# Forty of the experts' batch slots as seven-product items instead of group steps, in a kernel of shared and selected experts on one Trainium2 core

## The chip, the core and the metric

The kernel runs on one core of a Trainium2 chip. The metric is the device time of one execution in microseconds, as a median of several runs. The engines work side by side, each through its own list of instructions: PE (TensorE, matmuls), DVE (VectorE), ACT (ScalarE), POOL (GpSimd) and SP (SyncE, which here issues nearly all DMAs).

## What is computed

For 128 batches of 64 tokens with 256 features, two shared experts and one of five selected experts (hidden width 1024) are applied, mixed by a gate, added to the input, and then one diffusion step is made along both axes.

```python
def _dense(x, wi_, wo_):
    return jax.nn.relu(x @ wi_) @ wo_
...
s0 = _dense(x, swi[0], swo[0])
s1 = _dense(x, swi[1], swo[1])
wi_sel = wi[type_label]
wo_sel = wo[type_label]
h = jax.nn.relu(jnp.einsum('bsd,bdf->bsf', x, wi_sel))
eo = jnp.einsum('bsf,bfd->bsd', h, wo_sel)
gate_in = jnp.concatenate([eo[:, 0], s0[:, 0], s1[:, 0]], axis=-1)
w = jax.nn.softmax(jax.nn.relu(gate_in @ g1) @ g2, axis=-1)
...
return eo * w[:, 0] + s0 * w[:, 1] + s1 * w[:, 2]
```

Then `x = x + that`, and `x = x + zX*lap_x + zY*lap_y + zR*x*(1-x)`. The input has x in (128, 64, 256); `type_label` is one number per batch, known only at run time.

## The kernel before

**Precision.** Each fp32 operand is split into a high part (ACT copies it to a rounded type) and a low part (source minus high, on DVE or POOL; `split`, line 110). A product is three matmuls: high by high, high by low, low by high. In the second layer the high hidden part meets high and low weights in one matmul 512 wide, and the low hidden part meets the high weights in one 256 wide.

**Shared experts: items.** Tokens are taken as eight pairs of tiles; a tile is four steps of all 128 batches, 512 tokens, so a pair has 1024. An item n is one pair with one of the two shared experts (n = 2p + e, 16 items). An item has four units q, each for two of the eight hidden blocks of 128. A unit (`unit`, line 555) makes its 2 x 2 block product in seven block products in place of eight (Strassen-Winograd): the weight blocks A11, A12, A22 and sums S1 to S4, the token blocks B11, B21, B22 and sums T1 to T4, each times 3 matmuls, 21 matmuls of 512 columns per unit. The products go to PSUM tiles pa, pb and pd. pb takes several products one on top of the other, and between them ACT copies it out: to seed it from pa, then to u2, then to u3 (group `u` in the profile). TensorE's next product into pb waits for that copy.

Between the products of unit q stand "gaps": the second layer's matmuls of the preceding unit (`tile_a`) or, in unit 0, of the last rows 2 and 3 of the preceding item (`tile_b`, whose rows 0 and 1 stand at the item's end). `evacuate` (line 673) takes a finished row of 128 tokens out of PSUM: for items 0 and 1, ACT copies and DVE adds into the tiles `sh`, which stay in SBUF until the gate's weights exist; later items add onto yb.

Besides, a unit has four places for other work, its hooks. `at(k, ...)` (line 907) puts work at hook k, which is unit k // 4, place k % 4; 16 and 17 are after the last unit. Hook 0 of a unit stands behind its first gap, hook 1 behind the second gap, hook 2 behind the third. In order of the program a unit is: pa product, seed copy, gap, hook 0, S2 and A12 products, u2 copy and one hidden block, gap, hook 1, S3 and S1 products, u3 copy, gap, hook 2, A22 and S4 products, three more hidden blocks, hook 3.

ACT, DVE, POOL and PE keep the order of the program in this part (`in_order`, `keep_in_program_order`), and SP always does. A hook thus fixes where an instruction stands in the list of its engine. An engine may run ahead of the others as far as its own inputs allow, and if one instruction waits, all behind it on that engine wait too.

**Weights of items 0 and 1** come raw (`load_ws`) and are prepared on the fly: `prepare(u, k)` has POOL make S1 to S4 (`sum_wi`, four small sums) at k, splits the A blocks at k + 2 and the S blocks at k + 3 (`split_wi`), saves them to DRAM (`keep_wi`), and splits W-out at k + 4 (`split_wo`). The split W-out of all eight units stays in SBUF for the whole run (`wpool`). `again(0)` and `again(1)`, at hook 17 of items 0 and 1, prepare the first two units' S blocks, which item 0 did without. From item 2 on the split weights come back from DRAM (`load_wi`).

**Order of the batches.** `order_batches` (line 232), run in four steps at hooks of items 0 and 1, sorts the batches by expert into slots in units of four and writes a table `tab`: the batch of every slot and the expert of every unit of four. There are two classes: expert runs in eights come first, fours after. SP reads addresses from the table.

**Selected experts: groups.** After item 1, `stream` runs 19 groups that always exist: 14 of eight batches (512 tokens) and 5 of four. Two more run only if the table says so. A group uses plain products: 48 matmuls of 512 columns (`up`), then 32 of 512 and 32 of 256 (`down`); its results go to DRAM (`eo_d`). `load_group_x` (line 338) issues one DMA of 64 KB per batch. Group 0 is loaded at hook 12 of item 1 (`load_first_group`) and split at hook 16.

**Items 2 to 15** follow, with the gate in item 2, the results of the experts gathered from `eo_d`, and the diffusion in the hooks.

Of the kernel before, what the change touches and what calls it, by code (L numbers as in the profile page):

```python
# [8 lines left out]
F32 = mybir.dt.float32  # L9
# [7 lines left out]
P = 128  # L17
# [7 lines left out]
NBIG = (B // NB - NE + 2) // 2  # L25
NSURE = B // NB + 1 - 2 * NBIG
GROUPS = [(2 * NB * g, 2 * NB) for g in range(NBIG)] + [(u * NB, NB) for u in range(2 * NBIG, NU)]
# [6 lines left out]
LAG = 2  # L34
NWARM = 8
# [7 lines left out]
def cond_resid_kernel(ctx: ExitStack, tc: tile.TileContext, xg, xs, xn, itok, z, we, ws, g1, g2, out):  # L43
# [8 lines left out]

    nc = tc.nc
    const = ctx.enter_context(tc.tile_pool(name="const", bufs=1))
    wpool = ctx.enter_context(tc.tile_pool(name="wpool", bufs=1))
# [8 lines left out]
    eo_d = dram.tile([NSLOT * NT, ST * D], F32, name="eo_d")  # L64
    wi_d = [dram.tile([P, 2, 7, P], F32, name=f"wi_d{i}") for i in range(2 * NQ)]
# [56 lines left out]

    def split_wo(u):
        wop[u] = wpool.tile([P, 2, 2, D], F32R, name=f"wo{u}")
        split(wop[u][:, :, 0, :], wop[u][:, :, 1, :], wsr[u][:, :, 256:512], vec)

# [40 lines left out]

    def sum_x(p, i, eng):

        b11, b12, b21, b22 = (xraw[p, k, l] for k in range(2) for l in range(2))  # L170
        if i == T1:
            xsum[p, T1] = slot2(f"xt{p}_1")
            eng.tensor_tensor(xsum[p, T1], b12, b11, ALU.subtract)
        elif i == T2:
            xsum[p, T2] = slot2(f"xt{p}_2")
            eng.tensor_tensor(xsum[p, T2], b22, xsum[p, T1], ALU.subtract)
        elif i == T3:
            xsum[p, T3] = slot2(f"xt{p}_3")
            eng.tensor_tensor(xsum[p, T3], b22, b12, ALU.subtract)
        else:  # L180
            xsum[p, T4] = slot2(f"xt{p}_4")
            eng.tensor_tensor(xsum[p, T4], b21, xsum[p, T2], ALU.subtract)

    def split_x(p, i, eng):
        src = {B11: (0, 0), B21: (1, 0), B22: (1, 1)}
        src = xraw[(p,) + src[i]] if i in src else xsum[p, i]
        x = xop[p, i] = slot4(f"x{p}_{i}")
        split(x[:, 0, :], x[:, 1, :], src, eng)
# [43 lines left out]
    def order_batches():  # L232
# [7 lines left out]
        gps.memset(ones, 1.0)  # L240
        io_i = const.tile([P, NSLOT], I32, name="io_i")
# [22 lines left out]
        pad = const.tile([P, NE], F32, name="pad")  # L264
        vec.tensor_copy(pad, cntb)
        vec.tensor_scalar(cntb, cntb, -2 * NB, None, ALU.bitwise_and)

        big = const.tile([P, NE], F32, name="big")
        vec.tensor_copy(big, cntb)
        vec.tensor_sub(pad, pad, big)  # L270

        base = const.tile([P, 2 * NE + 1], F32, name="base")
        vec.memset(base, 0.0)
        for e in range(2 * NE):
            size = (big if e < NE else pad)[:, e % NE : e % NE + 1]
            vec.tensor_add(base[:, e + 1 : e + 2], base[:, e : e + 1], size)
        inbig = const.tile([P, NE], F32, name="inbig")
        vec.tensor_tensor(inbig, rank, big, ALU.is_lt)
        shift = const.tile([P, NE], F32, name="shift")
        vec.tensor_sub(shift, base[:, NE : 2 * NE], big)  # L280
        vec.tensor_add(rank, rank, shift)
        vec.tensor_sub(shift, base[:, 0:NE], shift)
        vec.tensor_mul(shift, shift, inbig)
        vec.tensor_add(rank, rank, shift)
# [20 lines left out]
        ge = [const.tile([1, NU], F32, name=f"ge{i}") for i in range(2)]  # L305
        cmp = const.tile([1, NU, NE - 1], F32, name="cmp")
        for i in range(2):
            b = base[0:1, i * NE + 1 : i * NE + NE]
            vec.tensor_tensor(
                cmp, first.unsqueeze(2).to_broadcast([1, NU, NE - 1]), b.unsqueeze(1).to_broadcast([1, NU, NE - 1]),  # L310
                ALU.is_ge,
            )
            vec.tensor_reduce(ge[i], cmp, AX.X, ALU.add)
        gt = const.tile([1, NU], F32, name="gt")
        vec.tensor_scalar(gt, first, base[0:1, NE : NE + 1], float(NE - 1), ALU.is_lt, ALU.mult)
        vec.tensor_add(ge[1], ge[1], gt)
        vec.tensor_tensor(tab[:, NSLOT : NSLOT + NU], ge[0], ge[1], ALU.min)

        vec.tensor_copy(tab[:, NSLOT + NU :], base[0:1, 2 * NE :])
# [18 lines left out]
    def load_group_x(g):  # L338
        skip = "the table's entries are bounded on the chip"
        s0, n = GROUPS[g]  # L340
        xr = group_tile(g, [P, n, 2 * S], F32, f"gxr{g}")
        for j0 in range(0, n, NB):
            _, vals = nc.values_load_multi_w_load_instructions(
                tab[0:1, s0 + j0 : s0 + j0 + NB], engines=(SP,), min_val=0, max_val=B - 1,
                skip_runtime_bounds_check_because=skip,
            )
            for j in range(NB):
                dma(xr[:, j0 + j, :], xg[bass.ds(vals[j], 1), :, :].rearrange("o p k -> p (o k)"))
        gxr[g] = xr

    def group_expert(g):
        s0 = GROUPS[g][0] // NB
        gval[g] = nc.values_load(
            tab[0:1, NSLOT + s0 : NSLOT + s0 + 1], engines=(SP,), min_val=0, max_val=NE - 1,
            skip_runtime_bounds_check_because="the table's entries are bounded on the chip",
        )
# [56 lines left out]

    def gate_shared():
        g = gate_in["s"] = small.tile([P, 4, P], F32, tag="s2", name="gis")
        pt = psum("pt_s")
        for i in range(4):
            tc.keep_in_program_order(
                nc.tensor.transpose(
                    pt[:, i * P : (i + 1) * P], sh[0, i // 2][:, 0, (i % 2) * P : (i % 2 + 1) * P], ident  # L420
                )
            )
        vec.tensor_copy(g.rearrange("p i c -> p (i c)"), pt)
# [112 lines left out]

    def product(dst, w, i, x, start, stop):
        for j, (wp, xp) in enumerate(((0, 0), (0, 1), (1, 0))):
            mm(dst, w[:, wp, i, :], x[:, xp, :], start and j == 0, stop and j == 2)
# [15 lines left out]
    def unit(n, q, gaps, hooks):  # L555
        p, e = divmod(n, 2)
# [47 lines left out]
    def plain_units():  # L604
# [20 lines left out]
        split_wo(0)  # L625
        sum_wi(2, gps)
# [3 lines left out]
        split_wo(1)  # L630
        split_wi(2, (0,))
# [9 lines left out]
    def row_work(n, l, i, fs, wide):  # L641

        p, e = divmod(n, 2)
        store = (ha, hb)[l]

        def one(f):
# [3 lines left out]
            h, wo = store[n, f], wop[e * NQ + f // 2][:, f % 2, :, :]  # L650
# [22 lines left out]
    def evacuate(n, l, i):  # L673
        p, e = divmod(n, 2)
        t = 2 * p + l
        acc = accs.pop((n, l, i))
        if p == 0:
            if (t, e) not in sh:
                sh[t, e] = pool4.tile([P, ST, D], F32, tag="t4", name=f"sh{t}_{e}")
            o = sh[t, e][:, i, :]  # L680
            act.activation(o, acc[:, 0, :], AF.Copy)
            vec.tensor_add(o, acc[:, 1, :], o)
        else:
            for half in (0,) if n == 2 * NP - 1 else (1, 0):
                add_y(t, acc[:, half, :], 1 + e, (i, i))

    def shared_item(n, before, bg):
# [168 lines left out]
    def ahead(g, f):  # L856
# [3 lines left out]
        if f == 0:  # L860
# [6 lines left out]
            if g + 1 < NRUN:  # L867
                if g < NBIG:
                    load_group_w(g + 1)
                load_group_x(g + 1)  # L870
            if g == NRUN - 2:
                load_x(1)
            if g == NRUN - 1:
                load_wi(2, 0)
                load_wi(2, 1)
        if f == 6 and NBIG <= g + 1 < NRUN - 1:
            load_group_w(g + 2)
# [34 lines left out]

    def prepare(u, k):
# [3 lines left out]
            at(k + 2, lambda: split_wi(u, (0,))),  # L917
            at(k + 3, lambda: split_wi(u, (1,)), lambda: keep_wi(u)),
            at(k + 4, lambda: split_wo(u)),
        )  # L920

    def again(u):

        sum_wi(u, vec)
# [6 lines left out]
    def order():  # L931
# [5 lines left out]
        at(10, lambda: split_wo(2)),  # L937
        at(11, lambda: load_ws(5)),
        at(14, order),
        at(16, lambda: sum_wi(4, vec), lambda: split_wi(4), lambda: keep_wi(4)),  # L940
        at(17, lambda: again(0), order),
    )
    left = shared_item(0, ([], []), bg)
    bg = join(
        at(0, lambda: load_ws(6), lambda: split_wo(4)),
# [6 lines left out]
        at(10, clear_spare, lambda: dma(g1t, g1), lambda: dma(g2t, g2)),  # L952
        at(12, load_first_group),
        at(16, lambda: split_group_x(0), *(lambda f=f: split_group_w(0, f) for f in range(FIRST))),
        at(17, lambda: again(1)),
    )
    wide, narrow = shared_item(1, left, bg)
# [64 lines left out]
    for p in range(1, NP):  # L1022
        ta, tb = 2 * p, 2 * p + 1
        for e in range(2):
            n = 2 * p + e
            parts = [ahead_w(n)]
            if n == 2:
# [6 lines left out]
                parts.append(at(6, gate_hidden_e, lambda: load_y(2)))  # L1034
                parts.append(at(8, lambda: load_eo(0)))
# [4 lines left out]
                parts.append(at(13, lambda: load_y(1)))  # L1040
                parts.append(starts(ta, 17, 0))
# [31 lines left out]
            left = shared_item(n, left, join(*parts))  # L1073
# [38 lines left out]
```

## Time and profile before

| | us |
|---|---|
| median of 3 runs (1059.9 to 1061.81) | 1060.4 |
| the profiled execution's own time | 1061.38 |
| its span, first to last instruction | 1059.6 |
| of it items 0 and 1, to the first group's first matmul | 94.1 |
| groups, 94.1 to about 458 | 363.9 |
| items 2 to 15, 458 to the end | 601.6 |

PE's granted clock is 0.999 of full. SP's DMAs take this long from issue to landing (medians): a batch of 64 KB 2.7 us, an expert's weights of 512 KB 4.9 us, split weights of 896 KB 4.7 us, yb of 512 KB 6.0 us, a result row of 128 KB 1.8 us.

The profile's rows are read as follows. A row of the windows view gives the length of a stretch, and for every engine how long it was busy in it with how many instructions. A timeline row gives start, duration, engine, line, operation, what is written and read, and how often; a bracket at its end is the time the engine stood idle before, and for whom. A row of a tile's group gives shortest, median and longest duration in ns. Line 82, 97 and 108 are the helpers through which all matmuls, all ordered vector work and all of SP's DMAs are recorded.

### The profile page before, as it was taken

The page shows a single profiled execution, that of the slowest core. Times are in us where ns is not written, and L with a number is a line of the kernel's source. Part 1 is how long each engine was busy: PE and PEld are TensorE (multiplying, and loading weights), DVE is VectorE, ACT ScalarE, POOL GpSimd, SP SyncE. Part 2 cuts the span into 40 slices and gives each one's busy share as a digit, 9 for nine tenths or more (in the row PEclk, how much of TensorE's full clock was granted, in tenths as well). Part 3 has the DMA queues.
Part 4 walks back from the last instruction along what each step waited for, and adds up shares of the span by engine and source line. Part 5 has one row for each costly group of instructions (what it writes and reads, how often), then busy time and mean ns, then how long its engine had stood idle before and what let it go on. Part 6 is the DMA issues. An engine that isn't in the chain of part 4 may idle for free.

```text
span 1059.6 us, 15690 instructions
## 1 busy us (share of the span) xinstructions
PE 1048.8 (99%) x5493; PEld 895.2 (84%) x5493; DVE 740.6 (70%) x1282; ACT 539.9 (51%) x996; POOL 220.7 (21%) x210
## 2 busy tenths in 40 slices
PE   9999999999999999999999999999999999999997
PEld 6878888888888889988888888888888888888887
DVE  7787655554545557748879768677687687696777
ACT  6566555544555456643545445445355364364362
POOL 3021101000010000321332322232242142053020
PEclk9999999999999999999999999999999999999999
DMA  5456543445434456635336334344253254244321
GB/s 174 142 183 227 191 147 120 139 143 171 145 120 139 155 163 208 220 132 193 122 115 216 120 120 164 121 152 164 84 191 130 73 206 149 80 166 161 111 75 45
DMA packets 66128, 155.72 MB, mean 147 GB/s; under 512 B 7584, under 2 KB 34464, under 8 KB 66048
## 3 DMA queue, kind: packets, MB, share of 16 engines
q1 hardware_dynamic: 63424, 145.78, 41.1%
q0 software_dynamic: 2480, 8.78, 2.3%
q8 instruction: 44, 0.72, 0.3%
q14 instruction: 36, 0.29, 0.1%
q10 hardware_dynamic: 144, 0.13, 0.0%
HBM read 129.77 MB, written 24.90 MB: 146 GB/s over the span
## 4 chain that ended last, share of the span: by engine, by line
PE 50%; DVE 5%; issue 1%; ACT 1%; DVEq 0%
PE acc L82 27%; PE pb L82 10%; PE pd L82 7%; PE pa L82 6%; DVE lq L97 2%; PE pu L82 1%; DVE pd L97 0%; DVE c L97 0%; DVE h_3a L97 0%; DVE h_5b L97 0%; DVE yb L97 0%; ACT h_3a L97 0%; PE pgs L82 0%; DVE la L97 0%; DVE end_q L97 0%
## 5 line engine op out<-in xcount | busy, mean ns | idle before, releaser
L82 PE MATMUL up<-gxh,gw 128*128 128x512 f32 (+1 forms) x608 | 179.6, 362 | 0.0
L82 PE MATMUL pb<-x,wi 128*128 128x512 f32 x549 | 157.5, 395 | 1.7 <-ACT pb L97 0.8
L82 PE MATMUL gacc<-gw,gh 128*128 128x512 f32 (+1 forms) x608 | 141.7, 375 | 0.0
L97 DVE SCALAR_TENSOR_TENSOR gl<-up,gh 128x512 fp32r<-128x512 f32 x112 | 77.1, 688 | 88.6 <-ACT gh L97 88.4
L97 ACT ACTIVATE gh<-up 128x512 fp32r<-128x512 f32 (+1 forms) x152 | 81.8, 539 | 109.2 <-PE up L82 108.4
L97 DVE TENSOR_TENSOR gw<-gwr,gw 128x512 fp32r<-128x512 f32 x152 | 104.7, 717 | 44.8 <-ACT gw L97 44.5
L82 PEld LDWEIGHTS gacc<-gw,gh 128*128 128x128 f32 x608 | 109.9, 188 | 20.9
L82 PEld LDWEIGHTS up<-gxh,gw 128*128 128x128 f32 x608 | 110.5, 189 | 16.5
L97 ACT ACTIVATE u<-pb 128x512 f32<-128x512 f32 x122 | 73.1, 599 | 92.2 <-PE pb L82 87.9
L82 PEld LDWEIGHTS pb<-x,wi 128*128 128x128 f32 x549 | 97.9, 189 | 22.4 <-ACT pb L97 3.1
L97 ACT ACTIVATE gw<-gwr 128x512 fp32r<-128x512 f32 x152 | 90.3, 631 | 50.2 <-POOL gxl L97 23.3
L97 DVE SCALAR_TENSOR_TENSOR yb<-acc,wgt,yb 128x256 f32<-128x256 f32 x216 | 99.4, 482 | 22.5 <-PE acc L82 18.8
L82 PE MATMUL up<-gxl,gw 128*128 128x512 f32 (+1 forms) x304 | 110.4, 363 | 0.0
L97 POOL TENSOR_TENSOR gxl<-gxr,gxh 128x1024 fp32r<-128x1024 f32 (+1 forms) x19 | 40.1, 2113 | 334.6 <-ACT gxh L97 298.0
L82 PE MATMUL pd<-x,wi 128*128 128x512 f32 x366 | 104.5, 394 | 0.8 <-DVE h_4b L97 0.2
L82 PE MATMUL pa<-x,wi 128*128 128x512 f32 x366 | 103.5, 391 | 0.9 <-PEq L963 0.9
L97 ACT ACTIVATE pb<-pa 128x512 f32<-128x512 f32 x61 | 35.5, 583 | 119.8 <-PE pa L82 118.8
L97 POOL TENSOR_TENSOR la<-yb 128x508 f32<-128x508 f32 (+1 forms) x28 | 31.8, 1134 | 281.5 <-ACT yb L97 280.0
L82 PEld LDWEIGHTS pd<-x,wi 128*128 128x128 f32 x366 | 68.0, 188 | 19.0 <-DVE c L97 3.7
L82 PEld LDWEIGHTS pa<-x,wi 128*128 128x128 f32 x366 | 67.7, 188 | 14.6 <-issue 1.1
L82 PEld LDWEIGHTS gacc<-gw,gl 128*128 128x128 f32 x448 | 61.1, 190 | 4.4
L97 DVE TENSOR_TENSOR c<-pd,u 128x512 f32<-128x512 f32 x61 | 42.0, 689 | 32.3 <-PE pd L82 17.6
(246 smaller groups left out, 2133.3 us busy)
## 6 DMA issues: line engine op xcount, KB each, us to landing
wi<-wi_d SPq DMA_DIRECT2D x55, 896.0 KB, 4.7
gwr<-we_in SPq DMA_DIRECT2D x72, 512.0 KB, 4.9
gxr<-xg_in SPq DMA_DIRECT2D x132, 64.0 KB, 2.7
xr<-xs_in SPq DMA_DIRECT2D x32, 256.0 KB, 5.2
eo_d<-ge SPq DMA_DIRECT2D x64, 128.0 KB, 1.8
yb<-xn_in SPq DMA_DIRECT2D x16, 512.0 KB, 6.0
y_out<-lq SPq DMA_DIRECT2D x30, 256.0 KB, 2.0
wi_d<-wi SPq DMA_DIRECT2D x8, 896.0 KB, 4.5
```

The source lines that it names most:

```text
L82: nc.tensor.matmul(out_ap, lhsT=lhsT, rhs=rhs, start=start, stop=stop, skip_group_check=True)
L97: ins = call(*args, **kwargs)
```

## The change

Ten of the 14 groups of eight become five "fours", each of sixteen slots (four units of four) with one expert, 1024 tokens. A four is run as an item, numbered n = 100 to 104 (`EI` = 100), between item 1 and the groups. The other four groups of eight and the groups of four stay. The table has three classes: sixteens, eights, fours.

- A four's x is loaded by `load_fours` as sixteen DMAs of a batch each, behind the read of the expert's number, into two tiles taken from the pool of yb. For the first four this is at hook 9 of item 1, for the others at hook 2 of the preceding four. The sums T1 to T4 are made on POOL at hooks 12, 13, 13, 14 of item 1, or 4, 5, 6, 7 of the preceding four. The splits B11, T2, B21, T3, T1, T4, B22 are at hooks 14, 15, 16, 16, 17, 17, 17 of item 1, or 8, 9, 10, 12, 16, 17, 17 of the four.
- Its weights are loaded raw (`load_we`), unit by unit, and prepared as in item 1. W-out and raw weights share a rotating pool of eight tiles.
- Its result rows are evacuated as in items 0 and 1 and sent to `eo_d`, one DMA a row.
- The shared experts' split W-out goes to DRAM (`keep_wo`) and returns in groups 2 and 3 (`load_wo`); the results `sh` of items 0 and 1 go to DRAM, and return in item 2 (`load_sh`, `load_row`).
- `again(0)` and `again(1)` move to the fifth step of groups 0 and 1, with their raw weights loaded once more (`reload`).

```diff
+NQUAD = (B // NB - 3 * NE + 3) // 4
+NPAIR = (B // NB - NE + 2) // 2
+NBIG = NPAIR - 2 * NQUAD
...
-    wpool = ctx.enter_context(tc.tile_pool(name="wpool", bufs=1))
+    wpool = ctx.enter_context(tc.tile_pool(name="wpool", bufs=8))
...
+    def load_raw(u, src):
+        wsr[u] = slotw(f"wsr{u}", [P, 2, 512], F32)
+        dma(wsr[u], src)
...
+    def keep_wo(u):
+        dma(wo_d[u], flat_wo(u))
+
+    def load_wo(u):
+        wop[u] = slotw(f"wo{u}", [P, 2, 2, D], F32R)
+        dma(flat_wo(u), wo_d[u])
...
+    def load_batches(s0, n, dst):
+
         for j0 in range(0, n, NB):
             _, vals = nc.values_load_multi_w_load_instructions(
                 tab[0:1, s0 + j0 : s0 + j0 + NB], engines=(SP,), min_val=0, max_val=B - 1,
...
             for j in range(NB):
-                dma(xr[:, j0 + j, :], xg[bass.ds(vals[j], 1), :, :].rearrange("o p k -> p (o k)"))
...
+                dma(dst(j0 + j), xg[bass.ds(vals[j], 1), :, :].rearrange("o p k -> p (o k)"))
...
+    def load_fours(n):
+
+        s0 = (n - EI) * 4 * NB
+        gval[n] = expert_of(s0)
+        xr = [opool.tile([P, ST + 2, D], F32, tag="yb", name=f"xr{n}_{l}") for l in range(2)]
+        xr = [t.rearrange("p r d -> p (r d)")[:, 0 : 4 * S * NB].rearrange("p (j c) -> p j c", c=2 * S) for t in xr]
+        load_batches(s0, 4 * NB, lambda j: xr[j // (2 * NB)][:, j % (2 * NB), :])
...
+    def load_sh(t):
+        for j in range(2):
+            sh[t, j] = pool4.tile([P, ST, D], F32, tag="t4", name=f"sh{t}_{j}")
+            dma(sh[t, j].rearrange("p s d -> p (s d)"), sh_d[2 * t + j])
...
     def evacuate(n, l, i):
...
+        if n >= EI:
+            o = small.tile([P, D], F32, tag="s2", name=f"eo{n}_{l}{i}")
             act.activation(o, acc[:, 0, :], AF.Copy)
             vec.tensor_add(o, acc[:, 1, :], o)
+            r0 = ((n - EI) * 4 * NB + l * 2 * NB) * S + i * P
+            dma(eo_d.rearrange("r (s d) -> (r s) d", d=D)[r0 : r0 + P, :], o)
...
+            if g < 2:
+                reload(g)
+            elif g < 4:
+                for u in range(NQ):
+                    load_wo((g - 2) * NQ + u)
...
+        if f == 5 and g < 2:
+            again(g)
...
+    def ready(u, k):
+
+        return at(k, lambda: sum_wi(u, vec), lambda: in_parts(u, (0, 1)))
...
-        at(16, lambda: sum_wi(4, vec), lambda: split_wi(4), lambda: keep_wi(4)),
-        at(17, lambda: again(0), order),
+        ready(4, 16),
+        at(17, order),
...
+    def next_fours(n, sums, splits):
+
+        return join(
+            *(at(k, lambda i=i: sum_x(n, i, gps)) for i, k in zip((T1, T2, T3, T4), sums)),
+            *(
+                at(k, lambda i=i: split_x(n, i, gps if i in (B11, B21, B22) else vec))
+                for i, k in zip((B11, T2, B21, T3, T1, T4, B22), splits)
+            ),
+        )
...
-        at(12, load_first_group),
-        at(16, lambda: split_group_x(0), *(lambda f=f: split_group_w(0, f) for f in range(FIRST))),
-        at(17, lambda: again(1)),
+        next_fours(EI, (12, 13, 13, 14), (14, 15, 16, 16, 17, 17, 17)),
+        ready(EI * NQ, 16),
+        at(16, lambda: load_we(EI, 1)),
     )
-    wide, narrow = shared_item(1, left, bg)
+    left = item(1, left, bg)
+
+
+    for n in range(EI, EI + NQUAD):
+        u = n * NQ
+        parts = [
+            at(0, lambda: out_parts(u)),
+            prepare(u + 1, 0),
+            at(1, lambda: load_we(n, 2)),
+            prepare(u + 2, 4),
+            at(5, lambda: load_we(n, 3)),
+            prepare(u + 3, 8),
+        ]
+        if n + 1 < EI + NQUAD:
+            parts += [
+                at(2, lambda: load_fours(n + 1)),
+                at(9, lambda: load_we(n + 1, 0)),
+                next_fours(n + 1, (4, 5, 6, 7), (8, 9, 10, 12, 16, 17, 17)),
+                ready(u + NQ, 16),
+                at(16, lambda: load_we(n + 1, 1)),
+            ]
+        else:
+            parts += [
+                at(12, load_first_group),
+                at(16, lambda: split_group_x(0), *(lambda f=f: split_group_w(0, f) for f in range(FIRST))),
+            ]
+        left = item(n, left, join(*parts))
```

## The prediction

> **What bounds the kernel now.** The first view is engine busy time, then the busy time by windows, which prices one stretch of each kind of work.
>
> ```profile
> PE 1048.8 (99%) x5493; PEld 895.2 (84%) x5493; DVE 740.6 (70%) x1282; ACT 539.9 (51%) x996; POOL 220.7 (21%) x210
> ```
>
> ```profile
> core 0: us, PE busy (x) PEld busy (x) DVE busy (x) ACT busy (x) POOL busy (x), PEclk, DMA share, GB/s
> 44.90:88.50 43.60, 43.18 (x216) 35.35 (x216) 34.82 (x93) 27.74 (x56) 7.91 (x10) 1.00 0.61 207
> 135.40:179.50 44.10, 44.10 (x227) 37.68 (x226) 23.42 (x40) 21.98 (x43) 4.81 (x2) 1.00 0.46 144
> 628.10:669.50 41.40, 41.40 (x215) 35.50 (x214) 30.77 (x51) 18.66 (x31) 6.33 (x7) 1.00 0.36 127
> 669.50:711.40 41.90, 41.77 (x214) 35.22 (x213) 32.15 (x51) 22.12 (x38) 16.78 (x14) 1.00 0.43 151
> ```
>
> TensorE is the bound at full clock. Row 135.40 is two whole groups of eight batches, without a gap: 22.05 us each. Rows 628.10 and 669.50 are items of seven products over as many tokens (1024). Row 44.90 is item 1, which also prepares its weights: it pays 2.2 us more than 41.4, with DVE busy for 34.8 of 43.6. So seven products are cheaper on TensorE, and what decides is whether the other queues deliver on time.
>
> The third view is the timeline of one item, whose first pa product starts at 586.4 (n = 5, third unit). I count from an item's first pa. In this third unit the first pa starts at +17.9, TensorE adds A22·T4 into pb at +24.1, and ScalarE must have copied pb out to u (609.09) before that.
>
> ```profile
> 607.67 0.60 ACT L97 ACTIVATE h_4a<-pa 128x512 fp32r<-128x512 f32 x1
> 609.09 0.60 ACT L97 ACTIVATE u<-pb 128x512 f32<-128x512 f32 x1 [0.82 <-PE pb L82]
> ```
> ```profile
> 604.29 0.84 PE L82 MATMUL pa<-x,wi 128*128 128x512 f32 x3
> ...
> 610.46 0.86 PE L82 MATMUL pb<-x,wi 128*128 128x512 f32 x3
> ...
> 613.66 0.85 PE L82 MATMUL pb<-x,wi 128*128 128x512 f32 x3
> ```
>
> ScalarE's instructions stand in program order. What hook 9 puts on it lies between these two rows, so if it waits, u waits, and TensorE with it. The slack is some 0.8 us.
>
> The fourth view is SP's own queue, and the group of POOL's sums.
>
> ```profile
> 75.85 5.61 SPq L108 DMA_DIRECT2D gxr<-xg_in  x8
> ...
> 95.89 5.02 SPq L108 DMA_DIRECT2D gxr<-xg_in  x8
> ```
> ```profile
> L97 POOL TENSOR_TENSOR xt<-xr,xr x14: 1283/1556/1792, 442.1 to 939.2; 128x512 f32<-128x512 f32 x14
> L97 POOL TENSOR_TENSOR xt<-xr,xt x14: 1288/1681/1788, 444.1 to 940.9; 128x512 f32<-128x512 f32 x14
> ```
>
> Eight batches keep SP for 5.0 to 5.6 us, each being a transfer of its own with an address read from the table. The first column of the POOL durations is its shortest, the middle its median: 1.56 and 1.68 us a sum.
>
> **The change, part by part.**
>
> *Products.* Two groups are 160 wide (512) and 64 narrow (256) matmuls; a four is 84 + 64 = 148 wide and 64 narrow. Starts are 0.227 us apart in wide runs (604.98, 605.20, 605.43) and 0.12 in narrow ones (609.51, 609.62). So 12 x 0.227 = 2.7 us go per four, which the windows confirm (44.1 - 41.4). Five fours: **-13.6 us**.
>
> *The fours' side work* (seven-block weights, x splits, first results copied, added and sent off). The ends: nothing beyond the clean item, or item 1's 2.2 us each. Nearest is row 669.50, which has the same seven x splits and four POOL sums on top of other DVE work and loses 0.5; item 1's excess contains the ordering chain, which fours have not. 5 x 0.5 = **+2.5 us** (0 to 11).
>
> *The next four's x, in fours 1 to 4.* Hook 2 issues sixteen batch loads on SP. Ahead of them in program order stand the two result transfers of the previous item's rows 2 and 3, whose narrow matmuls come in the gap just before hook 2. From the spacings above these end at +9.0; ScalarE's copy (0.39) and DVE's sum (0.42, the sh rows of item 1) bring +9.85, the transfer's issue (0.38) +10.2. The expert's number and the first addresses are read in some 0.7 us. Sixteen batches take 2 x 5.0 = 10.0 us: +20.9. The last lands 2.7 us later (median landing of gxr): **+23.6**. T1 needs all sixteen. POOL: T1 1.56, T2 1.68, so T2 exists at +26.8. Hook 9 has ScalarE split T2: 0.62, then u 0.60: +28.0. TensorE wanted to go on at +24.1: it stands for 3.9 us. Queued behind the same wait on POOL: T3 and T4 (3.2), then the four small sums of the item's own fourth unit's weights (0.46 each, 1.9): +31.9. Hook 11 splits them, ScalarE 0.63 and DVE 0.69: +33.2. The third of the S2 products in the fourth unit needs this at +27.8 (613.66 is +27.3). So the delay has grown to **5.4 us**; it contains the 3.9. The weights of that fourth unit queue on SP behind the sixteen batches as well (+21.3, and 4.9 to land: +26.2); that is before POOL comes to them, and costs nothing more. Ends: no load hiccup, shortest landing (1.7) and shortest sums: 2.5 us; the slower issue (11.2), a landing of 4 us and sums at 1.79 and 0.9: about 10 us. Four times 5.4: **+21.6 us** (10 to 40).
>
> *The same at the end of item 1*, for the first four. The ordering's last step ends at 70.1 now; its expert part gains five to six small operations of 0.2 to 0.3 us, 1.2 us together, so the table is there at 71.3, and SP reads the expert's number first. Reads 0.7, sixteen batches 10.0, landing 2.7: 84.7. T1 and T2: 88.0. ScalarE has hook 15's split of T2 before h_6b: 89.2. TensorE reads h_6b at 84.3 now. **+4.9 us** (2 to 8). Today no such wait exists: SP loads eight batches from 75.85, needed at hook 16.
>
> *Rest.* `again(0)` and `again(1)` leave the items for the groups, where DVE is busy 23.4 of 44.1 us; in item 1 this ends a pause of about 0.3 us at 47.3 behind again(0)'s splits: **-0.3**. Ordering has as many small steps as before up to the slots. `keep_wo`, `load_wo`, `reload`, `load_row`: eleven to twenty transfers of up to 512 KB in stages with a DMA share of 0.4 to 0.6, hooks ahead of their use. Where two groups loaded 2 MB of weights each, a four loads 2 MB once, which pays for them. `load_sh(0)` is issued near 478, behind load_wi, lands about 6 us later (as yb) and is used from about 485: nothing, up to 1.5 us if a second transfer delays it.
>
> The sum: -13.6 + 2.5 + 21.6 + 4.9 - 0.3 = **+15.1 us** on the span of 1059.6, so 1074.7, and 1076.5 with the 1.8 us around it. The median of the runs, 1060.4, is 1.0 below the profiled execution's own time, so **1075.5 us**.
>
> [...] The rows here say 0.63 to 0.70 us for each batch, issue and address together, so 10 us; I take the rows. [...]
>
> **Rivals.**
> - *x is in time* (faster side). If the sixteen loads land by +18.2, both waits vanish; it is decided there, 5.4 us before my landing. For it: the x loads of today's items (issued at 597.6, first used on POOL at 604.8) reach their splits in time, and POOL has little else to do. Against it: the two rows of SP. Then -13.6 + 2.5 - 0.3 gives **1049**.
> - *DVE and ScalarE are the bound*: every four runs like item 1 (2.2 us lost), the x loads cost nothing more, and item 1 keeps its time but for 1 us. -13.6 + 11 + 1 gives **1059**. For it: DVE's 80% in item 1. Against: that stage has the ordering chain, and the chain of SP is independent of it.
> [...]
> - A count that doesn't come about is no case: the item loop is unrolled, with 84 products per four.
>
> **Numbers.** Chances: forecast 0.74, x in time 0.13, engines 0.08, clock 0.05. The likeliest's own range is 1061 to 1090, its ends not all at once. To leave out no more than two in ten the range reaches down to **1052**, and ends at **1090**. About 0.2% (2 us) can be told from no change. Faster 0.18 (x in time, and part of the engines' case), same 0.03, slower 0.79.
>
> **What would show it.** In the profile after: items of a four 46 to 48 us long for the first four, about 42 for the fifth; POOL's xt sums waiting for DMA xr up to about +23; ScalarE's x split of T2 waiting for POOL, TensorE's pb waiting for ScalarE's u for about 4 us in each third unit and for wi in the fourth; SP with sixteen loads in 10 us; a pause of about 5 us just before the first four. If the fours' third units show no pause, or SP starts the loads before +9, the forecast is wrong; if fours are near 42 us throughout, the time is near 1050.

## The result and the profile after

The changed kernel takes **1071.54 us** (median of 4 runs, 1069.97 to 1073.38), the kernel before 1061.11 in the same comparison: 1.010 times as long, with an interval of 1.0078 to 1.0121. The forecast was 1075.5. The sign is right and the total is 4 us off, but the two stand on different ground: hardly one of the waits that were summed came about as it was told, and others took their place.

Spans are compared below: 1071.7 us after (its execution took 1073.38, the longest of the four), 1059.6 before. The engine rows first.

```profile
PE 1046.8 (98%) x5433; PEld 885.9 (83%) x5433; DVE 792.4 (74%) x1356; ACT 571.6 (53%) x1081; POOL 281.3 (26%) x305
```

TensorE has 60 matmuls less than before, as counted: 5 x 12. Its busy time fell by only 2.0 us, because some of its matmuls ran longer (behind the pause shown below 0.63 us in place of 0.39). DVE is busy for 52 us more and POOL for 61.

Then the five fours, one row each, cut at their first pa product. The eighth column is the granted clock.

```profile
core 0: us, PE busy (x) PEld busy (x) DVE busy (x) ACT busy (x) POOL busy (x), PEclk, DMA share, GB/s
89.00:137.30 48.30, 44.53 (x215) 36.08 (x214) 35.96 (x64) 30.02 (x62) 16.23 (x19) 0.96 0.31 99
137.30:184.20 46.90, 43.92 (x213) 36.10 (x213) 33.79 (x57) 28.62 (x59) 16.01 (x19) 0.96 0.30 90
184.20:229.50 45.30, 42.46 (x215) 35.09 (x214) 33.50 (x58) 28.52 (x59) 15.86 (x19) 1.00 0.31 94
229.50:276.20 46.70, 44.04 (x215) 36.21 (x214) 33.57 (x58) 28.63 (x59) 15.77 (x19) 0.96 0.29 90
276.20:318.30 42.10, 41.80 (x214) 35.16 (x213) 27.89 (x48) 28.27 (x56) 9.39 (x14) 1.00 0.39 124
```

The items of before that lose nothing start 41.35 us apart, 2.75 less than two groups (44.1); a four without a pause would take as long. The fours lose 7.0, 5.6, 3.9, 5.3 and 0.8 over that, 22.6 together, against 13.75 gained. They look nearly as foretold (46 to 48, the last 42). But in three of them the clock is at 0.96, which the forecast had at 1.00, and DVE is busier in the first four of them than in the fifth by 5.6 us or more, with nine or ten instructions more, or sixteen in the first.

In the second four (137.3 to 184.2), the forecast has A22·T4 wait for u at +24.1. Here is TensorE's timeline at its third unit, then DVE's, which it waits for, and POOL's.

```profile
157.70 0.61 PE L88 MATMUL pb<-x,wi 128*128 128x512 f32 x2
160.72 0.50 PE L88 MATMUL pb<-x,wi 128*128 128x512 f32 x1 [2.41 <-DVE wi L103]
161.06 0.92 PE L88 MATMUL pa<-x,wi 128*128 128x512 f32 x3
161.78 0.63 PE L88 MATMUL acc<-wo,h_3a 128*128 128x512 f32 x1
162.21 0.63 PE L88 MATMUL acc<-wo,h_2a 128*128 128x512 f32 x1
```
```profile
154.41 2.75 DVE L103 TENSOR_TENSOR wi<-wsr,wi 128x256 fp32r<-128x256 f32 x2
157.09 1.77 DVE L103 SCALAR_TENSOR_TENSOR h_3b<-c,h_3b 128x512 fp32r<-128x512 f32 x1
158.79 0.68 DVE L103 SCALAR_TENSOR_TENSOR h_3a<-pb,h_3a 128x512 fp32r<-128x512 f32 x1
...
159.99 0.69 DVE L103 TENSOR_TENSOR wi<-wsum,wi 128x512 fp32r<-128x512 f32 x1
```
```profile
152.92 1.30 POOL L103 TENSOR_TENSOR xt<-xr,xr 128x512 f32<-128x512 f32 x1 [7.71 <-DMA xr<-xg_in]
154.30 1.29 POOL L103 TENSOR_TENSOR xt<-xr,xt 128x512 f32<-128x512 f32 x1
155.54 1.48 POOL L103 TENSOR_TENSOR xt<-xr 128x512 f32<-128x512 f32 x1
156.98 1.33 POOL L103 TENSOR_TENSOR xt<-xr,xt 128x512 f32<-128x512 f32 x1
```

TensorE stands at +21.0 already, for the low part of the S blocks (`wi<-wsum`), which DVE makes. DVE has no bracket: it did not wait, its instructions took longer. The two small splits of the A blocks (256 and 128 columns, merged in one row that gives the first form) took 2.75 us and h_3b 1.77; in quiet stretches they take 0.62 and 0.69. Both lie beside POOL's four sums of x. POOL could start these at +15.6, eight microseconds ahead of the forecast's last landing (+23.6). ACT's split of T2, on which the forecast's wait hung, has no bracket either, so it did not wait for POOL:

```profile
162.59 0.64 ACT L103 ACTIVATE x<-xt 128x512 fp32r<-128x512 f32 x1
```

Behind the pause, the acc matmuls start 0.43 us apart in place of 0.227: here the array ran at half speed. This window of the same stretch shows the clock, again in the eighth column.

```profile
161.70:165.10 3.40, 3.40 (x9) 2.66 (x9) 1.61 (x3) 1.99 (x5) 1.36 (x1) 0.50 0.00 0
```

It costs some 1.6 us. Losses are counted here from start to start of the matmuls, over their usual 0.227; this gives a little more than the bracket, 2.7 in place of 2.41 for the pause above. So this four loses 0.66 us at the second unit's S2 product (DVE's wi again), 2.7 at the third's, 1.6 to the clock and 0.55 at the fourth's S2: 5.5 of its 5.6.

Why x is early stands in SP's timeline of the same four.

```profile
137.69 1.02 SPq L114 DMA_DIRECT2D eo_d<-eo  x2
139.31 0.34 SPq L114 DMA_DIRECT2D wsr<-we_in  x1
140.20 5.24 SPq L114 DMA_DIRECT2D xr<-xg_in  x9
146.39 0.33 SPq L114 DMA_DIRECT2D eo_d<-eo  x1
146.91 0.33 SPq L114 DMA_DIRECT2D xr<-xg_in  x1
147.35 0.39 SPq L114 DMA_DIRECT2D eo_d<-eo  x1
147.93 3.26 SPq L114 DMA_DIRECT2D xr<-xg_in  x6
```

Nine of the sixteen loads stand ahead of the first of the two late result transfers, from +2.9 on. The order of the instructions on SP is not that of the program's lines, though what stands ahead says that SP always keeps it: the loads with an address from the table stand further ahead in SP's list.

Over the whole run, the groups' first `up` comes 9.3 us later than in a kernel with only the five fours taken off the groups' time (94.08 + 10 x 22.05 = 314.6, against 323.9); the first four begins 0.5 later, the fours take 8.8. The groups take 0.2 less; item 2 adds 2.2, of which half clock from 472.3 to 475.7 is 1.6, and the rest of the run 0.8: 12.1.

### The profile page after: what moved, and what is told of

Its sections match the earlier page's. It is cut to its first block, busy times and chain, and to the rows that moved or that the text cites. A ratio compares the mean times of both kernels' runs of the same rounds, so it can differ in the third digit from the quotient of the medians.

```text
span 1071.7 us, 15763 instructions
## 1 busy us (share of the span) xinstructions
PE 1046.8 (98%) x5433; PEld 885.9 (83%) x5433; DVE 792.4 (74%) x1356; ACT 571.6 (53%) x1081; POOL 281.3 (26%) x305
## 4 chain that ended last, share of the span: by engine, by line
PE 50%; DVE 4%; issue 1%; ACT 1%; DVEq 0%; ACTq 0%
PE acc L88 26%; PE pb L88 10%; PE pd L88 6%; PE pa L88 6%; DVE lq L103 2%; PE pu L88 1%; DVE c L103 0%; DVE pd L103 0%; DVE h_3a L103 0%; DVE h_5b L103 0%; ACT h_3a L103 0%; PE pgs L88 0%; DVE yb L103 0%; ACT u L103 0%; DVE la L103 0%
## 5 line engine op out<-in xcount | busy, mean ns | idle before, releaser
L88 PE MATMUL pb<-x,wi 128*128 128x512 f32 x729 | 214.7, 400 | 14.1 <-DVE wi L103 12.1
L88 PEld LDWEIGHTS pb<-x,wi 128*128 128x128 f32 x729 | 131.2, 191 | 47.3 <-DVE wi L103 18.6
L103 ACT ACTIVATE pb<-pa 128x512 f32<-128x512 f32 x81 | 47.3, 584 | 123.5 <-PE pa L88 122.4
L103 POOL TENSOR_TENSOR x<-xr,x 128x512 fp32r<-128x512 f32 x33 | 45.9, 1393 | 130.8 <-ACT x L103 130.7
L88 PE MATMUL up<-gxh,gw 128*128 128x256 f32 (+1 forms) x288 | 74.0, 331 | 0.0
L88 PE MATMUL gacc<-gw,gh 128*128 128x512 f32 (+1 forms) x288 | 62.7, 360 | 0.0
L103 ACT ACTIVATE gh<-up 128x256 fp32r<-128x256 f32 (+1 forms) x72 | 34.2, 477 | 42.7 <-PE up L88 41.8
L88 PEld LDWEIGHTS gacc<-gw,gh 128*128 128x128 f32 x288 | 49.9, 188 | 8.4
L88 PE MATMUL acc<-wo,h_0b 128*128 128x256 f32 (+1 forms) x172 | 56.6, 333 | 0.2 <-DVE h_6b L103 0.2
L88 PE MATMUL acc<-wo,h_1b 128*128 128x256 f32 (+1 forms) x172 | 56.7, 334 | 0.0
L88 PE MATMUL acc<-wo,h_7b 128*128 128x256 f32 (+1 forms) x172 | 56.7, 334 | 0.0
L88 PE MATMUL acc<-wo,h_6b 128*128 128x256 f32 (+1 forms) x172 | 56.6, 333 | 0.0
L88 PE MATMUL acc<-wo,h_2b 128*128 128x256 f32 (+1 forms) x172 | 56.6, 333 | 0.0
L88 PE MATMUL acc<-wo,h_4b 128*128 128x256 f32 (+1 forms) x172 | 56.6, 333 | 0.0
```

The costliest lines, as they stand in the source:

```text
L88: nc.tensor.matmul(out_ap, lhsT=lhsT, rhs=rhs, start=start, stop=stop, skip_group_check=True)
L103: ins = call(*args, **kwargs)
```

## The experiments

The theory to be tested: **POOL's four sums of x, which read SBUF, hold DVE's two-input instructions; TensorE then waits for weights, and the pause drops its clock.** Against it: that the sums matter by their own length or by the x they deliver, that DVE is too full without them, and the recorded chain over SP. Each edit is made on the changed kernel.

**Without the sums.** The fours' T1 to T4 are left out, and the plain blocks B12 and B22 stand in for them in the products; nothing else goes.

```diff
+        if p >= EI:
+            xsum[p, i] = b12 if i in (T1, T2) else b22
+            return
...
-        like = by_batch if p >= EI and i in (B11, B21, B22) else (lambda ap: ap)
+        like = by_batch if p >= EI else (lambda ap: ap)
```

> Leaves out: POOL's four sums T1 to T4 of the fours' tokens (the splits read raw blocks instead). Everything on DVE, ACT, SP and PE stays. Port theory (POOL's sums hold up DVE's splits of two inputs, so the third unit's S weights come late): the pause of 2.3 to 2.6 us in the third unit of fours 1 to 4 and the half clock behind it go; DVE's two A splits take 0.6 us again and not 2.75; four starts 42.5 to 43 us apart; about 1071.5 - 4 x 3.9 = 1056 us. DVE-load theory (DVE simply has too much to do in a four, whoever else runs): DVE's list is the same, so the pause stays above 1.5 us; 1068 us or more. Recorded theory (x and its sums are late for ACT's split of T2): goes too, but the row before the pause would have to be ACT's u, not DVE's wi.

Measured: 1055.26 us, 0.9953 of before (0.9939 to 0.9967), so 16.3 below the change. The fours take 43.6, 42.9, 42.7, 42.7 and 42.1. DVE at the place of the 2.75:

```profile
148.31 0.62 DVE L103 TENSOR_TENSOR wi<-wsr,wi 128x256 fp32r<-128x256 f32 x2
149.09 0.69 DVE L103 SCALAR_TENSOR_TENSOR h_3b<-c,h_3b 128x512 fp32r<-128x512 f32 x1 [0.17 <-ACT h_3b L103]
```

The long pause and the half clock are gone; pauses of 0.66 us in the second unit and 0.53 in the fourth stay. The sums are the cause of two thirds of what the fours lose (22.6 - 7.3 = 15.3 us), but this alone does not tell whether by what they read, by their length, or by the x that they deliver.

**As long, but writing only.** In place of every sum, POOL reads eight columns of x (so that it waits for the loads just as long) and then writes zeros three times. The sums are left out of the products as above.

```diff
+            blank = slot2(f"blank{p}_{i}")
+            eng.tensor_copy(blank[:, 0:8].unsqueeze(2), b12[:, :, 0:1])
+            for _ in range(3):
+                eng.memset(blank, 0.0)
```

> Leaves out the same four sums; POOL instead waits for the same x (a copy of eight elements per partition) and then clears a tile of 512 columns three times for each, some 1.5 us in place of 1.3 to 1.5. So POOL is as busy at the same place, but reads almost nothing from SBUF. If what holds up DVE is that both read two inputs from SBUF (port theory): as e1, within 2 us, and DVE's A splits stay near 0.6 us. If any POOL work at that place delays DVE, or the order of POOL's list alone delays the S sums of the fourth unit: as the changed kernel, 1068 to 1072.

Measured: 1056.31 us, 0.9960 of before (0.9946 to 0.9974), like the kernel without sums. POOL's timeline in the second four (from 131.0), then DVE's:

```profile
146.76 0.19 POOL L103 COPY blank<-xr 128x8 f32<-128x8 f32 x1 [7.78 <-DVE h_2a L103]
147.02 1.70 POOL L103 MEMSET blank<- 128x512 f32 x3
```
```profile
148.18 0.62 DVE L103 TENSOR_TENSOR wi<-wsr,wi 128x256 fp32r<-128x256 f32 x2
148.96 0.69 DVE L103 SCALAR_TENSOR_TENSOR h_3b<-c,h_3b 128x512 fp32r<-128x512 f32 x1 [0.17 <-ACT h_3b L103]
```

POOL is occupied at the same place (+15.8) for longer than by the sums (1.9 us each against 1.3 to 1.5), and DVE's two splits beside it take 0.62. Thus it is not POOL's occupation or its position, but what it reads; and not the x that it delivers, for which ACT's split of T2 did not wait in the changed kernel.

**The sums later.** A version that computes everything: the four sums at hooks 12, 12, 13, 13, their splits behind them.

```diff
-                next_fours(n + 1, (4, 5, 6, 7), (8, 9, 10, 12, 16, 17, 17)),
+                next_fours(n + 1, (12, 12, 13, 13), (8, 14, 10, 15, 16, 17, 17)),
```

> Same work, the four sums at hooks 12, 12, 13, 13 of the preceding four instead of 4 to 7, and T2 and T3 split at 14 and 15. Port theory: the sums then meet a stretch in which DVE has no weights to split, the third unit's pause goes, ACT or DVE waits a little at hook 14; fours 42.5 to 43.5 apart, 1055 to 1060 us. DVE-load theory: the pause in the third unit stays, 1067 or more. If x's arrival were the cause, it goes as well.

Measured: 1057.05 us, 0.9962 of before (0.9947 to 0.9976). The first four fours take 44.0, 42.6, 42.6 and 42.7, without half clock. The sums run from 158.86 in the second four, directly behind the split of x that POOL still has, and again a DVE instruction meets POOL's work there (h_5b, 1.50 us), but behind it nothing is short of time. Being held is no loss by itself; it is one where TensorE needs what follows.

**Weights sooner.** The other way to the same end: the sums stay, and the fours' weights are split one hook earlier, to give DVE room.

```diff
+    def sooner(u, k):
...
+            at(k, lambda: sum_wi(u, gps)),
+            at(k + 1, lambda: in_parts(u, (0,))),
+            at(k + 2, lambda: in_parts(u, (1,))),
+            at(k + 4, lambda: out_parts(u)),
...
-            prepare(u + 1, 0),
+            sooner(u + 1, 0),
```

(`prepare(u + 2, 4)` and `prepare(u + 3, 8)` likewise.)

> Same work; in the fours the A blocks of a unit's weights are split one hook after its S sums and the S blocks two hooks after, in place of two and three. Theory that the S blocks come just in time on DVE's list: the small pauses of about 0.6 us in the second and fourth unit of every four go (10 x 0.6 = 6 us), and the third unit's S split stands ahead of most of the collision with POOL, so its pause shrinks below 1 us as well: 1050 to 1056. If the pauses come from the amount of work and not its order: 1070.

Measured: 1064.91 us, 1.0032 of before (1.0019 to 1.0044); 1050 to 1056 was expected, so this missed. The fours take 46.2, 44.2, 44.9 and 45.7, at full clock. Apart from 0.2 us at the start of the first four, TensorE no longer waits for wi. In these four fours it waits for c (2.7 us in all) and, longer, for ACT's u (6.7). DVE's, ACT's and TensorE's rows in the second four:

```profile
152.29 1.77 DVE L103 SCALAR_TENSOR_TENSOR h_3b<-c,h_3b 128x512 fp32r<-128x512 f32 x1
...
158.56 1.78 DVE L103 TENSOR_TENSOR wi<-wsr,wi 128x256 fp32r<-128x256 f32 x2
160.26 0.68 DVE L103 TENSOR_TENSOR x<-xt,x 128x512 fp32r<-128x512 f32 x1
160.86 0.68 DVE L103 TENSOR_TENSOR c<-pd,u 128x512 f32<-128x512 f32 x1
```
```profile
155.30 0.60 ACT L103 ACTIVATE h_2b<-pd 128x512 fp32r<-128x512 f32 x1 [1.04 <-DVE pd L103]
```
```profile
157.48 0.96 PE L88 MATMUL pb<-x,wi 128*128 128x512 f32 x3 [0.67 <-ACT u L103]
...
161.60 0.96 PE L88 MATMUL pd<-x,wi 128*128 128x512 f32 x3 [0.82 <-DVE c L103]
```

The weights' splits now stand ahead of c, the sum that frees pd, and meet POOL there (its low part of an x block, 1.30 us from 158.56). And h_3b is held beside the sums; DVE's pd behind it is late, ACT's h_2b waits for pd, and u stands behind h_2b on ACT. Whatever DVE has queued behind a held instruction is late: wi before, c and pd now. The splits' place was the right cure only once the sums were elsewhere.

**Both.** The last two edits together.

> Same work; the late sums and the weight splits one hook sooner together. Port theory with just-in-time S splits: the sums no longer meet the splits, so the two small pauses of a four (0.6 us each) go without new ones: fours 41.5 to 42.2 apart, 5 x 1.2 us below the version with late sums alone: 1050 to 1053. If splits made sooner only push back the hidden blocks behind them on DVE whatever POOL does, as in the run with sooner splits alone: no better than late sums alone, 1057 or more.

Measured: **1052.51 us** (1051.52 to 1052.84), 0.9914 of before (0.9901 to 0.9928): faster than both kernels. Windows of the second and third four:

```profile
131.30:173.00 41.70, 41.70 (x215) 35.26 (x214) 30.95 (x58) 28.42 (x59) 16.21 (x19) 1.00 0.33 101
173.00:214.60 41.60, 41.60 (x213) 35.13 (x213) 30.69 (x57) 28.41 (x59) 16.18 (x19) 1.00 0.34 102
```

All the instructions of the change, POOL's 19 a four too, fit beside TensorE; it is busy throughout, and these two are within 0.35 us of 41.35. What the change lost in the fours was a matter of places, apart from some 1.4 us at the start of the first.

**The recorded chain, forced.** For the recorded theory x has to be as late as it said. Two small ACT writes into x's tiles, put at hook 2 ahead of the loads, hold all sixteen back.

```diff
+        if n > EI:
+            for t in xr:
+                act.activation(t[:, :, 0:1], ident[:, 0:8].unsqueeze(2), AF.Copy)
```

> Same work, but the x loads of fours 2 to 5 really stand where the recorded sum put them: each x tile is first touched by a small ACT copy at hook 2, behind the copies of the previous item's rows 2 and 3, so SP can't issue before +10. Recorded sum: last x near +23.6, POOL's first sum starts there; ACT's split of T2 waits for it, TensorE waits for ACT's u some 4 us in the third unit, in all 5.4 us a four beside the 1.2 of small pauses, and pauses of 4 us let the clock drop each time (1.6 us): fours 48 to 50 apart, 1075 to 1082 in all. If arrival doesn't matter and only the meeting of POOL and DVE does: the sums meet other DVE work than today, fours stay at 45 to 47: 1068 to 1073.

Measured: 1071.24 us, 1.0094 of before (1.0079 to 1.0109), at full clock. SP's timeline, ACT's and TensorE's in the second four, which begins at 135.8:

```profile
144.93 1.28 SPq L114 DMA_DIRECT2D eo_d<-eo  x2
146.81 9.22 SPq L114 DMA_DIRECT2D xr<-xg_in  x16
```
```profile
160.76 0.63 ACT L103 ACTIVATE x<-xt 128x512 fp32r<-128x512 f32 x1 [2.05 <-POOL xt L103]
161.29 0.58 ACT L103 ACTIVATE u<-pb 128x512 f32<-128x512 f32 x1
```
```profile
161.93 0.96 PE L88 MATMUL pb<-x,wi 128*128 128x512 f32 x3 [0.96 <-ACT u L103]
...
167.35 1.13 PE L88 MATMUL pb<-x,wi 128*128 128x512 f32 x3 [1.41 <-ACT pb L103]
```

With sixteen loads from +11.0, every link of the recorded chain is there: T2, ACT's split, u, pb, and the fourth unit after it. But the first four fours take 45.9 to 47.3 us, where 48 to 50 and 1075 to 1082 in all were expected of this chain; the total lies in the range written for the other theory, and it is the waits that show the chain. This four loses 4.6 us, of which 0.65 is the second unit's small pause, so the chain costs 3.9 rather than 5.4: TensorE loses 1.7 us at and around the first pb (recorded: 3.9), since x is there at +22.3 in place of +23.6, a sum takes 1.3 us, not 1.6, and TensorE itself arrives later; the fourth unit loses 1.9. That the total equals the change's is a coincidence: the change without this chain pays by holding and clock instead. The recorded mechanism is possible, and did not happen.

**The change once more**, for the spread of the clock drops.

> The changed kernel once more, for its granted clock. Clock theory: each pause of 2.3 to 2.6 us in a third unit either sets off 3.4 us at half clock (1.6 us lost) or not, by where it falls; fours with a drop are 46.5 to 47 apart, fours without 45 to 45.5, and which fours drop may differ from the first profile. If the four without a drop differed by something else, the same four (the third) is short again and no other.

Measured: 1069.22 us, a single execution. Its windows of the second, third and fourth four:

```profile
136.20:183.10 46.90, 44.00 (x215) 36.18 (x214) 33.81 (x58) 28.62 (x59) 15.78 (x19) 0.96 0.30 91
183.10:228.10 45.00, 42.41 (x215) 34.99 (x214) 33.22 (x58) 28.51 (x59) 15.88 (x19) 1.00 0.31 95
228.10:273.10 45.00, 42.39 (x215) 35.00 (x214) 33.22 (x58) 28.51 (x59) 15.87 (x19) 1.00 0.31 94
```

The fourth is 45.0 too, at full clock, where it was 46.7 at 0.96 in the first profile. Same code, one drop less, and which four has it is not fixed. Fours with and without a drop differ by 1.7 to 1.9 us, but their pauses are not equal; by the starts of the matmuls a drop is worth 1.6. In the first profile the third four stood idle for 2.26 us without a drop, the second for 2.41 with one.

The records show a difference between the two: where the pause lies. By the clock records in the trace of the first profile, the granted clock is 0.50 from 113.94, 161.72, 253.88 and 472.33, for 3.41 us each. These starts are 47.79, 92.16 and 218.45 us apart: 14, 27 and 64 times 3.413 us, to 0.01 us. The two drops in the fours of this execution (113.29 and 161.07) are 47.78 us apart, again 14 times. So in each of the two profiles the starts lie on one grid of 3.41 us, though the pauses before them do not. Two stretches of this grid in the first profile, in the second and in the third four (third column: TensorE's busy time):

```profile
158.30:161.70 3.40, 0.99 (x5) 0.84 (x5) 3.34 (x6) 1.59 (x4) 2.61 (x5) 1.00 0.02 5
206.10:209.50 3.40, 1.95 (x8) 1.61 (x9) 2.69 (x5) 2.56 (x6) 2.56 (x4) 1.00 0.00 0
```

In the second four the whole pause (158.31 to 160.72) lies in one stretch. In the third an edge of the grid, at 206.09, cuts the pause (205.29 to 207.55), and this is the emptier of the two stretches. The three drops in third units of the first profile follow a stretch with 1.0 to 1.3 us of TensorE's work; of the other stretches in its five fours the emptiest is the one with 1.95 us, and no drop followed it. That is four pauses of one profile; the drop in item 2 came after 2.0 us of work, and no run was made to test how work and drop hang together.

## Why the prediction was right in sign and wrong in mechanism

- **"-13.6" for the products** held: 60 matmuls fewer, and a four near 41.35 us when nothing waits (41.6 to 41.8 in the version with both edits).
- **The failed step: "Ahead of them in program order stand the two result transfers of the previous item's rows 2 and 3".** It is so in the program, not in SP's list: the loads began at +2.9, not +10.2, and the last was in by +15.6, not +23.6. With it fell the 3.9, the 5.4 and the sum of 21.6. The time for x on SP, 10.0 us, was near (about 9 in three stretches, the transfers between them left out). The forecast said that a start before +9 makes it wrong; that is what happened, though not with the 1049 of its rival "x is in time".
- **What took its place**: POOL's sums were priced only by what they cost POOL (1.56 and 1.68 us), never by what they do to others, in the forecast and in "x is in time" alike. They held DVE; TensorE lost 2.4 to 2.7 us by it in each of the first four fours (10.3), and in three of them the clock fell (4.8). The kernel without sums confirms this sum of 15.1: its fours are 15.3 us shorter. The trace before had shown the effect: in the item of 586.4, POOL works from 604.84 to 612.5 without a gap (four sums, then a low part of x), and DVE's h_5b beside it, at 611.38, took 1.67 us in place of 0.69.

```profile
611.20 1.31 POOL L97 TENSOR_TENSOR x<-xr,x 128x512 fp32r<-128x512 f32 x1
```
```profile
611.38 1.67 DVE L97 SCALAR_TENSOR_TENSOR h_5b<-c,h_5b 128x512 fp32r<-128x512 f32 x1 [0.70 <-ACT h_5b L97]
```

What the runs show of this: the splits took 0.62 us beside 1.7 us of memsets and 2.75 beside sums. They read two tiles in SBUF, and so does h_3b, which ended 0.55 us after POOL's last sum (158.86 and 158.31 in the second four), as if it had waited for it. h_3a, which has one of its inputs in PSUM (pb), took its usual 0.68 beside POOL's next instruction, and DVE's sums `c` and `pd`, which read pd in PSUM, took 0.67 to 0.69 us in all 162 cases of the changed kernel's profile, where h_3b and h_5b (median 0.69) took up to 1.78. What inside the chip holds the instruction was not shown.

- **"2.5" for the side work** was low: without sums the fours still lose 7.3 us, within the 0 to 11 that the term allowed. Most of it is small waits for DVE's wi in the second and fourth unit (0.66 and 0.53), and 0.7 at the start of the first four (1.4 with the sums). Splitting the weights a hook earlier, with the sums moved away, removes the former; the row from which 0.5 was taken had prepared no weights.
- **"4.9" at the end of item 1**: the first four begins 0.5 us later. There too loads stand ahead in SP's list (four at 63.80, though the ordering's last step ends at 70.3, twelve from 69.84), and POOL's first sum starts at 79.95, not about 85. The longer ordering cost a pause of 0.7 us near 70.7, which was not in the sum.
- **The clock** is in none of the sum's terms, though it has 0.05 among the chances and pauses of 3.9 us were expected. In the first profile it dropped after 2.39, 2.41 and 2.12 us of idle time by the brackets, for 3.41 us each, and not after 2.26 in the third four; nor did it after the pauses of 0.96 and 1.41 in the kernel with forced x. Each drop cost about 1.6 us; three of them in the fours and one in item 2 were missing.
- **"Nothing" for what follows the fours**: 2.8 us came, 1.6 of them by a drop in item 2, after short pauses at its start (0.72, 0.44 and 0.23 us).

So -13.75 by products, +10.3 by pauses at the sums, +4.8 by clock, +7.3 by small waits, +0.5 in item 1 and +2.8 later give +11.95, beside the 12.1 of the spans. The 21.6 + 2.5 forecast for the fours stand against 22.6 measured from other causes. That the total nearly came out is luck.

**Left open.** What set off the drop in item 2: it begins on the same grid, but TensorE was busy for 2.0 us in the stretch before it, with no pause longer than about 0.7 us by the records. The start of the first four and the ordering's longer path were not tried alone. And why the loads are put ahead of the results in SP's list was not examined; only that they are.

## What to carry to other kernels

An instruction added to an engine that has time to spare is still to be priced on its neighbours: look in the trace for the longest durations of the busy engine's instructions and at what ran beside them, before a POOL job is called free. Read the order of a DMA queue from the trace, not from the program, where addresses come from registers. Once an instruction is held, what counts is what stands next on its engine: move the one that holds to where nothing behind is due, then the one that is due, and measure both together, as one alone may lose.

## What the hardware showed unexpectedly

- POOL's sums of 512 columns stretched two DVE splits of 256 and 128 columns together from 0.62 to 2.75 us and a 512-wide low part from 0.69 to 1.77; memsets of like length stretched neither.
- In the changed kernel's first profile TensorE's clock fell to half for 3.41 us after pauses of 2.39, 2.41 and 2.12 us, at about 1.6 us each, and not after one of 2.26 us; in another execution of it, in two of the four such places. The four drops of the first profile start whole multiples of 3.413 us apart. The three in its fours came where TensorE had worked for 1.3 us or less in the stretch of this grid before, and none where it had worked for 1.95.
